# One change in four places of a fused attention block: sums moved between engines, sums left to DMA, transpositions moved later

## The chip, the cores and the metric

The kernel runs on one NeuronCore of a Trainium2 chip. The time is the device time of one execution in microseconds; lower is better. The core has five engines with instruction queues of their own, which run in order: TensorE (PE in the profile; its weight loads are PEld), VectorE (DVE), ScalarE (ACT), GpSimd (POOL) and SyncE (SP), which here only issues DMAs. GpSimd issues DMAs too. Both DMA queues share 16 DMA engines.

## The reference

For x of 2 batches x 1024 tokens x 1024 channels, all in float32:

```
xn  = layernorm(x)
qkv = clip(xn @ Wqkv.T, -8, 8);  q, k = layernorm(q)*w+b, layernorm(k)*w+b
att = softmax(q k' / sqrt(32) + slope_h * (kpos - qpos), causal) v     (32 heads of 32)
out = x + att @ Wout.T + xn @ (alpha * sign(Wffn)).T + bias
```

alpha is the mean of |Wffn| along a row.

## The kernel before

**Seven products.** Each 1024 x 1024 projection (k, q, v for each batch, and the output projection) is done for two token tiles of 128 at a time with seven products of blocks instead of eight. The weight matrix has blocks 11, 12, 21, 22 of 512 x 512, each held as 4 pieces (c = 0 to 3) of 128 x 512; from them come the sums t1 to t4 (`plan_difference`, L217 to L230). The token side has the quarters A11, A12 (first tile) and A21, A22 (second tile), and the sums S1 to S4 (`add_up`, L361 to L370: four operations of 128 x 512 on GpSimd). `seven` runs the blocks in the order 11, 21, t2, t3, t4, t1, 22: four accumulated matmuls each, with two records in the profile for one (L377). Blocks 11 and 21 need no sum of the second tile; t2 needs S2. `combine` adds the products up on VectorE (L396).

**Weights** go through a ring of 28 buffers of 128 x 512. A list `todo` holds loads, sums and stores in order; `load_weights(n)` gives it room for n more buffers, one after each matmul of the last pair of a projection. The first batch computes the sums (on GpSimd; t1 and t2 of the very first weights, k0, on VectorE) and stores them to DRAM right behind (`plan_store`, L236); the second batch loads them. The sums of Wout (o) are computed on GpSimd too, during the last tile of the binary layer.

**Pieces and sides.** `pieces()` yields the projections, the binary layer and the output projection in small pieces. Every second piece advances the generators in `sides`: normalizations (`layernorm`, `to_channels`, both with two empty yields between the last step of the normalization and the transposition on PE), the constants, and loads. `yield` thus fixes the distance in the queues, not in time.

**Attention** runs in 169 steps. A block is a batch, a half of the queries (qb = 0 or 1) and a group of four heads. For each block the first scores (L832) give the maximum of each query (VectorE, L849). `shifts` then has two halves: seven small GpSimd operations that make `shift_b` from the maxima (L865 to L871), and one step later four PE transpositions (`trs`, L876) and a ScalarE copy to `rows`. Nine steps behind, the second scores (L891, with `rows` added by L904) are masked on VectorE (L917), exponentiated on ScalarE (L926) and added up for the denominators on GpSimd (L942); the products with the values (L956) come one step later. A unit of second scores is one or two key tiles. A block of qb = 0 has 3 units and one of qb = 1 has 7; the first unit of a block has no sums on GpSimd, and the unit with two tiles (384 + 128 queries) has eight.

One step, as it stands in the program (L1039 to L1056): first scores; second half of `shifts` of the block that closed a step ago; first half of `shifts` of a block that closes now; division of a finished block (den, L975); pieces; products with the values; second scores; pieces. All engines run their queues in this order.

**The binary layer** (`binary_linear`) first takes |W| and sign(W) on ScalarE, two buffers ahead of the matmul that makes alpha (L601). Then for each of 16 token tiles: x and bias are added on GpSimd (L623), the product (L651) is scaled on VectorE to `fo` (L663), added to it on GpSimd in two halves (L664), and the row is stored to `out` (L666). The split of the tokens into two float32r parts needs two VectorE subtractions of SBUF operands for a tile (`hl`, L633). **The output projection** adds its rows to `out` with an adding DMA on GpSimd's queue (L725).

Of the kernel before, what the change touches and what calls it, by code (L numbers as in the profile page):

```python
# [25 lines left out]
def parallel_block_kernel(  # L26
# [36 lines left out]
    nc = tc.nc  # L63
# [134 lines left out]

    W = {}
# [17 lines left out]
    def plan_difference(what, to, a, b, c):  # L217


        def do():  # L220
            less = W[what, b, c]
            if to == "t3":
                w = W.pop((what, b, c))
            else:
                w = wpool.tile([P, HALF], FP, tag="w", name=f"w_{what}_{to}_{c}")
            eng = nc.vector if what == "k0" and to in ("t1", "t2") else nc.gpsimd
            eng.tensor_tensor(w, W[what, a, c], less, ALU.subtract)
            W[what, to, c] = w

# [11 lines left out]
    def plan_weights(what, src, e0, first, again):  # L241


        def part_of(block, c):
            r = ((int(block[0]) - 1) * NI + c) * P
            return src[r : r + P, e0 : e0 + D][:, half(int(block[1]) - 1)]

        if not first:
            for block in ORDER:
                for c in range(NI):  # L250
                    if block[0] == "t":
                        at = lambda name=f"{what[0]}{block}{c}": kept[name]
                    else:
                        at = part_of(block, c)
                    plan_load(what, block, c, at)
            return
        for block in ("11", "21"):
            for c in range(NI):
                plan_load(what, block, c, part_of(block, c))
        start = what == "k0"  # L260
        if start:
            for c in range(NI):
                for block in ("12", "22"):
                    plan_load(what, block, c, part_of(block, c))
        for c in range(NI + 2):
            if c < NI and not start:
                for block in ("12", "22"):
                    plan_load(what, block, c, part_of(block, c))
            if 0 < c <= NI:
                plan_difference(what, "t1", "12", "11", c - 1)  # L270
                plan_difference(what, "t2", "22", "t1", c - 1)
                plan_difference(what, "t3", "22", "12", c - 1)
            if again and c > 1:
                for to in ("t1", "t2", "t3"):
                    plan_store(what, to, c - 2)
        for c in range(NI + 1):
            if c < NI:
                plan_difference(what, "t4", "21", "t2", c)
            if again and c > 0:
                plan_store(what, "t4", c - 1)  # L280

    for b in range(B):
        for what, e0 in (("k", D), ("q", 0), ("v", 2 * D)):
            plan_weights(f"{what}{b}", wqkv_t, e0, b == 0, b == 0)
# [16 lines left out]
    plan_weights("o", wout_t, 0, True, False)  # L301
# [59 lines left out]
    def add_up(pr, eng, c0, c1):  # L361
# [5 lines left out]
        eng.tensor_tensor(at(S1), at(A21), at(A22), ALU.add)  # L367
        eng.tensor_tensor(at(S2), at(S1), at(A11), ALU.subtract)  # L368
        eng.tensor_tensor(at(S4), at(A12), at(S2), ALU.subtract)
# [21 lines left out]
    def combine(name, ra, rb, ready):  # L391

        h = {}

        def plus(dst, ps, other):
            nc.vector.tensor_tensor(dst, ps, other, ALU.add)  # L396

        def take(block, ps):
# [12 lines left out]
            elif block == "t1":  # L411
                plus(rb[:, half(1)], ps, h.pop("u3"))
                plus(h["u"], ps, h["u"])
# [53 lines left out]
    def turn_x(b, t):  # L467
# [13 lines left out]
        else:  # L481
            nc.gpsimd.dma_start(d[:, 0], pr[:, A21])
            add_up(pr, nc.gpsimd, 0, NI)
# [4 lines left out]
    def layernorm(b, t):  # L488
        yield from normalize_x(b, t)
        yield 0.0  # L490
        yield 0.0
# [9 lines left out]
    def to_channels(what, b, t, raw, par, at, d):  # L501
# [3 lines left out]
        yield 0.0  # L505
        yield 0.0
# [13 lines left out]
    def projected(what, b, ready):  # L520

        if what == "k":
            if b == 0:
# [5 lines left out]
                yield from normalize_x(b, 1)  # L529
            yield from turn_x(b, 0)  # L530
            if b == 0:
                load_weights(RING - 4 * NI)
        for p in range(NT // 2):
# [16 lines left out]
            yield from seven(pr, name, f"{what}{b}", not more, take, ORDER[:2])  # L550
            if what == "k":
                if p == 0:
                    yield from turn_x(b, 1)
                if more:
                    sides.append(layernorm(b, 2 * p + 3))
            assert ("x", b, p) in done
            yield from seven(pr, name, f"{what}{b}", not more, take, ORDER[2:])
# [8 lines left out]

    def values(b):
        def ready(t, rows):
# [9 lines left out]

    def binary_linear():
# [5 lines left out]
        ab = pair_tile("alpha_bias").rearrange("p k c q -> p (k c q)")  # L585
# [523 lines left out]
```

## Time and profile before

| | us |
|---|---|
| median of 3 runs | 1741.54 (1733.9 to 1747.48) |
| the profiled execution | 1737.78 |
| its span, first to last instruction | 1736.0 |
| PE busy | 1640.9 (95%) |
| GpSimd busy | 1052.9 (61%) |
| VectorE busy | 958.0 (55%) |
| ScalarE busy | 691.1 (40%) |
| DMA, mean over the span | 127 GB/s |
| mean granted clock of TensorE | 0.969 |

How the stages lie in the span: k, q and v of the first batch to about 365 us, without attention until 303; attention from there, with k, q and v of the second batch among it to 1005; magnitudes of the binary layer to 1050; its tiles to about 1365; the output projection to 1728. The profile gives for each engine its busy time, and for the idle time before an instruction what released it. Issuing a DMA is not counted as busy. A granted clock of 0.5 in a stretch means that PE ran at half speed for all of it. Records of PE are pipelined: a group of matmuls listed as 2.04 us x8 may hold overlapping ones.

### The profile page before, as it was taken

The page shows a single profiled execution, that of the slowest core. Times are in us where ns is not written, and L with a number is a line of the kernel's source. Part 1 is how long each engine was busy: PE and PEld are TensorE (multiplying, and loading weights), DVE is VectorE, ACT ScalarE, POOL GpSimd, SP SyncE. Part 2 cuts the span into 40 slices and gives each one's busy share as a digit, 9 for nine tenths or more (in the row PEclk, how much of TensorE's full clock was granted, in tenths as well). Part 3 has the DMA queues.
Part 4 walks back from the last instruction along what each step waited for, and adds up shares of the span by engine and source line. Part 5 has one row for each costly group of instructions (what it writes and reads, how often), then busy time and mean ns, then how long its engine had stood idle before and what let it go on. Part 6 is the DMA issues. An engine that isn't in the chain of part 4 may idle for free.

```text
span 1736.0 us, 25493 instructions
## 1 busy us (share of the span) xinstructions
PE 1640.9 (95%) x8480; PEld 691.5 (40%) x8480; DVE 958.0 (55%) x2782; ACT 691.1 (40%) x1425; POOL 1052.9 (61%) x1292
## 2 busy tenths in 40 slices
PE   3999999989999999999999998999989799999998
PEld 1444444433443333333333334545544333333343
DVE  4454352656666755666555556666776355555222
ACT  2442431125565445554433364444433243433420
POOL 7427043125654475557566667787887998777851
PEclk8999999999999999999999998899999899999999
DMA  7347475571325612336222434343332312331332
GB/s 285 146 160 270 134 245 183 188 268 66 141 74 178 222 59 76 104 104 224 61 80 98 152 134 151 111 134 121 133 106 86 103 28 77 97 74 20 87 59 48
DMA packets 108867, 220.83 MB, mean 127 GB/s; under 512 B 9856, under 2 KB 50304, under 8 KB 105664
## 3 DMA queue, kind: packets, MB, share of 16 engines
q1 hardware_dynamic: 87808, 139.24, 24.2%
q0 software_dynamic: 20928, 79.97, 14.2%
q8 instruction: 67, 1.10, 0.2%
q14 instruction: 64, 0.52, 0.1%
HBM read 139.74 MB, written 79.43 MB: 126 GB/s over the span
## 4 chain that ended last, share of the span: by engine, by line
PE 75%; DVE 8%; POOL 7%; issue 5%; ACT 3%; DMA 2%; SPq 0%; POOLq 0%; DVEq 0%; ACTq 0%
PE s L891 9%; PE s L832 9%; PE o L956 7%; PE mm_v_t L377 7%; PE mm_q_t L377 7%; PE mm_k_t L377 6%; PE mm_f L651 6%; PE mm_o_t L377 5%; PE mm_v L377 4%; PE mm_q L377 4%; PE mm_o L377 3%; POOL pT L942 2%; PE mm_k L377 2%; PE den L975 2%; PE s L904 2%
## 5 line engine op out<-in xcount | busy, mean ns | idle before, releaser
L942 POOL TENSOR_TENSOR pT<-pT,pT 128x512 f32<-128x512 f32 (+3 forms) x640 | 597.4, 958 | 171.0 <-ACT pT L926 160.3
L926 ACT ACTIVATE pT<-s,kpos 128x512 f32<-128x512 f32 (+3 forms) x768 | 379.6, 588 | 486.1 <-DVE s L917 287.1
L849 DVE CUSTOM_DVE_ANT_0 sumss<-s,rel 128x512 f32<-128x512 f32 (+3 forms) x512 | 302.3, 591 | 183.2 <-PE s L832 129.4
L832 PE MATMUL s<-kg,qg 32*128 32x512 f32 (+3 forms) x1536 | 206.4, 531 | 4.1 <-ACT pT L926 3.4
L891 PE MATMUL s<-qg,kg 32*128 32x512 f32 (+3 forms) x1536 | 196.5, 533 | 12.3 <-DVE mx L849 11.8
L917 DVE TENSOR_TENSOR s<-s,behind 128x128 f32<-128x128 f32 x512 | 123.8, 293 | 104.0 <-PE s L904 99.3
L956 PE MATMUL o<-pT,vg 128*32 128x512 f32 (+3 forms) x1536 | 159.9, 504 | 0.0
L651 PE MATMUL mm_f<-sg,hl 128*128 128x512 f32 x512 | 146.8, 426 | 2.8 <-ACT hl L630 2.4
L832 PEld LDWEIGHTS s<-kg,qg 32*128 32x128 f32 x1536 | 82.7, 186 | 129.9 <-issue 47.6
L891 PEld LDWEIGHTS s<-qg,kg 32*128 32x128 f32 x1536 | 76.0, 186 | 132.3 <-DVE mx L849 70.6
L377 PE MATMUL mm_k_t<-w_k_t,xT 128*128 128x512 f32 x224 | 110.1, 613 | 17.8 <-POOL xT L368 17.8
L989 POOL TENSOR_TENSOR o<-o,inv 128x512 f32<-128x512 f32 x31 | 39.4, 1272 | 139.9 <-ACT inv L984 139.8
L651 PEld LDWEIGHTS mm_f<-sg,hl 128*128 128x128 f32 x512 | 94.6, 197 | 63.2 <-issue 32.6
L377 PE MATMUL mm_q_t<-w_q_t,xp 128*128 128x512 f32 x224 | 107.6, 607 | 0.0
L377 PE MATMUL mm_v_t<-w_v_t,xp 128*128 128x512 f32 x224 | 106.1, 606 | 0.0
L377 PE MATMUL mm_k<-w_k,xT 128*128 128x512 f32 x192 | 99.3, 655 | 3.4 <-ACT xT L475 3.4
L849 DVE CUSTOM_DVE_ANT_0 umss<-s,rel,mx 128x512 f32<-128x512 f32 (+2 forms) x96 | 59.3, 617 | 63.1 <-PE s L832 52.6
L377 PE MATMUL mm_o_t<-w_o_t,ot 128*128 128x512 f32 x192 | 93.2, 610 | 0.0
L377 PE MATMUL mm_o<-w_o,ot 128*128 128x512 f32 x192 | 93.0, 612 | 0.0
L377 PE MATMUL mm_v<-w_v,xp 128*128 128x512 f32 x192 | 91.8, 611 | 0.0
L377 PE MATMUL mm_q<-w_q,xp 128*128 128x512 f32 x192 | 91.4, 604 | 0.0
L849 DVE CUSTOM_DVE_ANT_0 sumss<-s,rel,mx 128x512 f32<-128x512 f32 (+2 forms) x96 | 59.3, 617 | 48.2 <-PE s L832 37.7
(164 smaller groups left out, 1974.4 us busy)
## 6 DMA issues: line engine op xcount, KB each, us to landing
xp<-xd SPq DMA_DIRECT2D x16, 1792.0 KB, 7.6
kg<-kd SPq DMA_DIRECT2D x48, 256.0 KB, 4.8
vg<-vd SPq DMA_DIRECT2D x48, 256.0 KB, 5.1
xd<-xT POOLq DMA_DIRECT2D x8, 1280.0 KB, 4.9
x<-in_x_dram SPq DMA_DIRECT2D x16, 512.0 KB, 6.7
kd<-kT POOLq DMA_DIRECT2D x16, 512.0 KB, 4.1
qd<-qT POOLq DMA_DIRECT2D x16, 512.0 KB, 4.1
qg<-qd SPq DMA_DIRECT2D x32, 256.0 KB, 4.4
```

The lines of the kernel that those rows point to most:

```text
L377: nc.tensor.matmul(ps, pr[:, FACTOR[block], c, :], W[what, block, c], start=(c == 0), stop=(c == NI - 1),)
L651: nc.tensor.matmul(ps, hl[c // NI][:, m % 2, c % NI, :].bitcast(FR), sg[n, c], start=(m == 0), stop=(m == 2 * NC - 1),)
L832: nc.tensor.matmul(banks[j][:, c0 : c0 + n], q[r, tokens(i - qb * NQ)], k[r, :n], start=True, stop=True,)
L849: nc.vector.tensor_tensor_reduce(out=sums[:, :n], in0=banks[j][:, c0 : c0 + n], in1=rel[:, o0 : o0 + n], scale=1.0, scalar=LOWEST if k0 == ...
L891: nc.tensor.matmul(banks[j][:, c0:c1], k[r, tokens(kt % NQ)], q[r, q0:], start=(c0 == 0), stop=False,)
L904: nc.tensor.matmul(banks[j][:, c0:c1], ones_b[r, :], rows[r, q0:], start=False, stop=(c1 == HALF or (kt, q0) == unit[-1]),)
L917: nc.vector.tensor_tensor(at, at, behind, ALU.add)
L926: nc.scalar.activation(pT[:, c0:c1], banks[j][:, c0:c1], AF.Exp, bias=kpos[:, h, a : a + 1], scale=slopes[h],)
L942: nc.gpsimd.tensor_tensor(part_sum, part_sum, pT[:, c0:c1], ALU.add)
L956: nc.tensor.matmul(po[32 * j : 32 * j + 32, q0:], v[:, kt % NQ, 32 * j : 32 * j + 32], st["pT", name, j][:, c0:c1], start=opening, stop=la ...
L975: nc.tensor.matmul(ps[32 * j : 32 * j + 32, :], ones, st.pop(("sum", b, qb, g, j)), start=True, stop=True,)
L989: nc.gpsimd.tensor_tensor(ot, ot, inv, ALU.mult)
```

## The change

1. The sums change sign: weights are only added (t1 = 11 + 12, t2 = 22 + t1, t3 = 22 + 12, t4 = 21 + t2), and the token side and two of the combinations subtract instead. The number of operations stays.
2. The stores of k0's sums are put behind the first four loads of q0. Those of q0 and v0 stay.
3. The token sums of the very first pair go to VectorE. The second tile of a batch's first pair is transposed after block 11 instead of after 21, and the second tile's normalization comes after the first tile's transposition.
4. A third empty yield stands before the transpositions of normalized rows.
5. The sums of Wout are made in DRAM, by four copies and seven adding DMAs of 1 MB on GpSimd's queue, and all seven blocks are loaded.
6. x is copied to `out` by 16 DMAs on SP's queue, and bias is added by 16 adding DMAs on GpSimd's queue, both from the start of v0 on as a side; the binary layer's `fo` is added by 32 adding DMAs. x and bias are not loaded any more, and the additions L623 and L664 and the stores L666 go.
7. Magnitudes are taken three ahead, into larger buffers.
8. In the last block, the sums of key tiles 5 to 7 go to VectorE.
9. In each step both halves of `shifts` come after the second scores.

```diff
@@ plan_difference, now plan_sum
-            eng.tensor_tensor(w, W[what, a, c], less, ALU.subtract)
+            eng.tensor_tensor(w, W[what, a, c], more, ALU.add)
@@ plan_weights, now plan_first (batch 0) and plan_again (batch 1 and o)
+        start = what == "k0"
         for block in ("11", "21"):
             for c in range(NI):
-                plan_load(what, block, c, part_of(block, c))
+                put(block, c)
+            while later:
+                plan_store(*later.pop(0))
...
-            if again and c > 1:
+            if c > 1:
                 for to in ("t1", "t2", "t3"):
-                    plan_store(what, to, c - 2)
+                    later.append((what, to, c - 2))
+            while later and not start:
+                plan_store(*later.pop(0))
...
-    plan_weights("o", wout_t, 0, True, False)
+    plan_again("o", wout_t, 0)
@@ add_up
-        eng.tensor_tensor(at(S1), at(A21), at(A22), ALU.add)
+        eng.tensor_tensor(at(S1), at(A21), at(A22), ALU.subtract)
         eng.tensor_tensor(at(S2), at(S1), at(A11), ALU.subtract)
-        eng.tensor_tensor(at(S4), at(A12), at(S2), ALU.subtract)
+        eng.tensor_tensor(at(S4), at(A12), at(S2), ALU.add)
@@ turn_x
-            add_up(pr, nc.gpsimd, 0, NI)
+            add_up(pr, nc.vector if (b, p) == (0, 0) else nc.gpsimd, 0, NI)
@@ layernorm and to_channels
-        yield 0.0
-        yield 0.0
+        for _ in range(3):
+            yield 0.0
@@ projected
                 yield from normalize_x(b, 0)
-                yield from normalize_x(b, 1)
             yield from turn_x(b, 0)
             if b == 0:
+                yield from normalize_x(b, 1)
                 load_weights(RING - 4 * NI)
...
-            yield from seven(pr, name, f"{what}{b}", not more, take, ORDER[:2])
-            if what == "k":
-                if p == 0:
-                    yield from turn_x(b, 1)
-                if more:
-                    sides.append(layernorm(b, 2 * p + 3))
+            args = pr, name, f"{what}{b}", not more, take
+            yield from seven(*args, ORDER[:1])
+            if what == "k" and p == 0:
+                yield from turn_x(b, 1)
+            yield from seven(*args, ORDER[1:2])
+            if what == "k" and more:
+                sides.append(layernorm(b, 2 * p + 3))
@@ new: a side, appended at the start of values(0)
+    def beside():
+        yield from residual()
+        yield from output_weights()
+    def residual():
+        for b, t in every_tile:
+            nc.sync.dma_start(out[b, tokens(t), :], x[b, tokens(t), :])
+            yield 0.0
+        for _ in range(12):
+            yield 0.0
+        for b, t in every_tile:
+            nc.gpsimd.dma_start(
+                out[b, tokens(t), :], bias.partition_broadcast(P), accum_op=ALU.add
+            )
+            yield 0.0
+            yield 0.0
+    def output_weights():
+        parts = {
+            "t1": ("11", "12"),
+            "t2": ("22", "11", "12"),
+            "t3": ("12", "22"),
+            "t4": ("21", "22", "11", "12"),
+        }
+        full = {}
+        for n in range(4):
+            for to, of in parts.items():
+                if n >= len(of):
+                    continue
+                src = block_of(wout_t, 0, of[n])
+                if n == 0:
+                    full[to] = dram.tile([HALF, HALF], FP, tag=f"wo{to}", name=f"wd_o{to}", bufs=1)
+                    nc.gpsimd.dma_start(full[to], src)
+                else:
+                    nc.gpsimd.dma_start(full[to], src, accum_op=ALU.add)
+                yield 0.0
+            for _ in range(8):
+                yield 0.0
...
@@ binary_linear
-        magnitude(0)
-        magnitude(1)
+        for a in range(3):
+            magnitude(a)
...
-            xr = io_tile(f"xr_{b}_{t}")
-            nc.sync.dma_start(xr, x[b, tokens(t), :])
             yield 0.0
-            nc.gpsimd.tensor_tensor(xr, xr, bias_bc, ALU.add)
...
                 nc.vector.tensor_tensor(fo, ps, alpha[:, half(n)], ALU.mult)
-                nc.gpsimd.tensor_tensor(xr[:, half(n)], xr[:, half(n)], fo, ALU.add)
+                nc.gpsimd.dma_start(out[b, tokens(t), half(n)], fo, accum_op=ALU.add)
                 yield SHORT
-            nc.gpsimd.dma_start(out[b, tokens(t), :], xr)
@@ second_scores
-                nc.gpsimd.tensor_tensor(part_sum, part_sum, pT[:, c0:c1], ALU.add)
+                late = (b, qb, g) == blocks[-1] and kt > NT // 2
+                eng = nc.vector if late else nc.gpsimd
+                eng.tensor_tensor(part_sum, part_sum, pT[:, c0:c1], ALU.add)
@@ the main loop
-        for c in chains:
-            next(c, None)
-        chains = []
-        if n in closes:
-            chains.append(shifts(*closes[n]))
-            next(chains[-1])
         m = n - LAG
...
             second_scores(*second[m])
+        for c in chains:
+            next(c, None)
+        chains = []
+        if n in closes:
+            chains.append(shifts(*closes[n]))
+            next(chains[-1])
         fill(free * (1.0 - BEFORE))
```

## The prediction

> **What bounds the kernel now.** I read the page first: TensorE (PE) is busy for 95% of the span, the next engine, GpSimd (POOL), for 61%. So the change can win only what PE loses: its stops, and half clock after them. The chain of waits, for PE alone, gives the stops:
>
> ```profile
> PE mm_k_t L377 <- POOL xT L368: 17.8, 2, 14.8
> PE tr_x L448 <- ACT x L443: 13.9, 5, 8.3
> PE s L891 <- DVE mx L849: 11.8, 8, 3.9
> PE den L975 <- POOL pT L942: 11.3, 1, 11.3
> PE trs L876 <- POOL shift_b L869: 10.6, 5, 5.7
> PE ps_a L601 <- ACT absw L592: 5.7, 3, 2.6
> ```
>
> Columns: total us, times, longest. One stop of 14.8 us is the token sums of the first pair; 11.3 us is a denominator waiting for a GpSimd queue that had fallen behind. The table of stretches of 50 us then says where GpSimd is the limit (columns: length, busy PE, PEld, DVE, ACT, POOL, clock, DMA share, GB/s):
>
> ```profile
> 1250.00:1300.00 50.00, 44.33 (x290) 22.22 (x291) 36.95 (x90) 22.14 (x42) 44.35 (x43) 0.97 0.36 127
> 1300.00:1350.00 50.00, 46.10 (x268) 22.35 (x268) 30.56 (x68) 17.56 (x32) 40.82 (x38) 0.89 0.24 80
> 1350.00:1400.00 50.00, 38.66 (x228) 15.05 (x226) 19.41 (x56) 14.72 (x29) 48.02 (x52) 0.86 0.31 101
> ```
>
> GpSimd works 41 to 48 us of each 50, and PE has its worst stretches there, at a lowered clock. Last the timeline, around one closing block of the first batch:
>
> ```profile
> 871.85 0.40 PE L904 MATMUL s<-rows,ones_b 3*128 3x384 bf16 x8
> 874.92 6.02 POOL L942 TENSOR_TENSOR pT<-pT,pT 128x384 f32<-128x384 f32 x8
> 876.92 0.40 PE L876 MATMUL trs<-ident_b,shift_b 128*128 128x128 bf16 x4
> 880.56 0.29 PE L904 MATMUL s<-rows,ones_b 3*128 3x256 bf16 x4
> ```
>
> A step's second scores end at 872.25, its eight sums on GpSimd at 880.94, the next step's second scores at 880.85. Remember these three times.
>
> **First pair's sums: -12.5 us.** PE stands from 26.66 to 41.44, because GpSimd does the 16 weight stores, the k0 sums and constants first, and S1 and S2 (1.27 us each) only from 38.78. Now VectorE does them. What is late next: the copies of the second tile's transposition on ScalarE, which queue behind the third tile's Ln at 23.48 (0.29), its Exp (0.20) and one PSUM copy (0.58), so they end at about 25.8. The four t4 sums on GpSimd, no longer parted by stores, fill about 22.3 to 27.4, and a VectorE sum of two SBUF operands can wait such a run out (shown below at line 633), so S2 ends near 28.8 (0.69 each). 41.4 - 28.9 = 12.5; bounds -16 (no waiting) and -9 (another GpSimd run).
> The 16 stores move to the first loads of q0 (120 to 140 us), where DMA is already busy for its whole time (share 0.99 and 1.04 in two stretches of 10 us). 4 MB more at 360 to 390 GB/s are 11 us; q0's t2 sums end 4 us before PE wants them, the t4 sums are just in time: **+3** (0 to +7).
>
> **Transpositions a yield later: -5 us.** The stops at 70, 72, 100, 101, 155, 255 and 260 us, together 5.5 us, wait for a normalized row (bounds 0 and -5.5). Behind them only the sums for the next pair come later, with 9 us to spare.
>
> **Residual and bias in DRAM: +4 us.** 16 copies on SP's queue fit in the empty DMA slices at 290 to 300 and 320 to 330. The 16 bias adds on GpSimd's queue fall at about 316 to 370. An adding DMA of 512 KB lands in 5.2 us against 3.2 for a plain one (rows out_dram from or and from xr), and its 4096-byte packets take 397 ns in the mean in the last 60 us, plain ones 160: 128 x 0.397/16 = 3.2 us of all engines each. k1's 7 MB of weights and its x tiles load at 340 to 370, at a DMA share of 0.86 to 1.0; PE already stops 5.0 us there. Moving the second tile's transposition one block forward helps by up to 5; late loads cost up to 15. I take +4, by the row of the full DMA. The eleven 1 MB DMAs for Wout come at about 370 to 560 (share 0.36 over the first batch), needed after 1005: nothing; if GpSimd had to wait for one, up to 3 us each inside the same bound.
>
> **Magnitudes three ahead: -4 us** of the 5.7 us of ps_a and the 10.2 us at half clock from 1044.7 (5.1 lost; bounds 0 and -8).
>
> **GpSimd relieved, 1050 to 1400 us: -33 us.** Out go the bias sum (16 x 2.49 = 39.8 us), the residual sum (32 x 1.33 = 42.5), 16 stores (9.2) and 16 Wout sums (16 x 1.27 = 20.3); in come 32 adding DMAs at the 0.86 us of line 725 (27.5): 84 us less. What PE loses there:
>
> ```profile
> 1333.01 8.44 DVE L633 TENSOR_TENSOR hl<-xt,hl 128x512 fp32r<-128x512 f32 x2
> 1333.03 2.37 POOL L623 TENSOR_TENSOR xr<-xr,alpha_bias 128x1024 f32<-128x1024 f32 x1
> 1335.37 4.93 POOL L942 TENSOR_TENSOR pT<-pT,pT 128x512 f32<-128x512 f32 x4
> 1341.91 1.85 PE L891 MATMUL s<-qg,kg 32*128 32x512 f32 x2 [3.90 <-DVE mx L849]
> ```
>
> Two subtractions that take 0.68 each alone stand 8.4 us while GpSimd runs, then PE waits 3.9. Stops of this kind: 3.42, 0.90, 1.53, 3.90 and the denominator's 11.34, 21.1 together; half clock follows them for 10.2, 6.8, 3.4, 6.8 and 13.7 us, a loss of half, 20.5. Of 41.6 I take 80%, since runs of four or eight sums (5 to 6 us) stay (bounds -41 and -17). A half-tile fo is now free only when its DMA has landed: 0.86 + 5.2 us, under the 19 us until its buffer returns.
>
> **The main loop's chain: +51 us.** Both halves of `shifts` move behind `second_scores`. So the seven small GpSimd operations (2.1 us from 865's start to the last 869's end) stand behind that step's sums, and PE's transposition behind the next step's second scores. In the block shown: sums end 880.94, shift_b 883.0, PE is there at 880.5: it stands 2.5 us. It is in order; behind it wait the next fills and scores, and ScalarE's copy of rows. I worked this for all 32 blocks, with the step's own sums: blocks of the first half of the queries follow an opening unit without sums and have 5 to 14 us to spare. The first batch's eight late blocks stand 1.8, 0.1, 1.9, 2.9, 0, 2.5, 1.8, 2.4; the two after them 0.5, 0.8; the second batch's, with GpSimd's backlog taken out up to 1365 us, 1.6, 2.0, 2.8, 2.6, 3.2, 3.0, 4.9, 7.0 (the last two behind four sums of `add_up`). 42 in all, for today's 10.6: +31.
> Then the clock. Stops of 2.4 us and more here are followed by half clock six times in seven, shorter ones from 1 us four times in ten, mostly for 6.8 us. Nine long and five short ones of the eighteen: 9 x 0.85 x 3.4 + 5 x 0.4 x 3 = 32, less today's 5, and rounded down since three of the twelve slow stretches last only 3.4 us: **+20**. Bounds of the whole: 0 (shift_b in time, by the rows of the early blocks) and +74 (42 - 10.6 + 14 x 3.4 - 5).
>
> ```profile
> 408.38 1.53 PE L891 MATMUL s<-qg,kg 32*128 32x512 f32 x3 [1.06 <-DVE mx L849]
> ```
>
> ```profile
> 410.00:417.00 7.00, 7.00 (x14) 2.18 (x15) 4.11 (x15) 3.55 (x5) 2.27 (x8) 0.53 0.45 188
> ```
>
> After a stop of 1.06 us (timeline) the granted clock is 0.53 of full speed for 7 us (table of stretches). The Trainium skill ("TensorE: Matmul & The Clock Gate", "HAM oscillation — how this bites in real kernels") gives as its rule that gaps longer than about 3.4 us are to be avoided. By that rule only two stops of the chain would slow the clock, its term would be about +2 instead of +20, and the sum 18 us lower; the row speaks against it.
>
> **Last sums on VectorE: 0.** The last denominators at 1675.47 follow a matmul without a stop, and GpSimd's sums end at 1671.36. 12 sums by 0.69 fit; behind GpSimd runs they could cost 3.
>
> **Sum.** -12.5 + 3 - 5 + 4 - 4 - 33 + 51 = +3.5 on the profiled execution's 1737.8 (span 1736.0), so 1741.3. The median of the runs, 1741.5, lies 3.8 above that execution: **1745 us** as such a median.
>
> **Rivals.**
> A, slower: the stop at shift_b with its clock. Place: PE's transposition in the 18 blocks with sums ahead. Price: all fourteen stops over 1 us pay 3.4 us of clock, 48 instead of 25, so +23: 1768 (own range 1759 to 1795, as the stops themselves may be a third longer). From a chain cost of 65 us on it decides for slower by over 1%. For it: six of seven long stops did pay. Against: nine of the eighteen are under 2.4 us.
> B, faster: GpSimd, relieved, and VectorE, quicker at the masks that the exponentials wait for, bring shift_b in time; the chain costs nothing: 1694. For it: two of the first eight late blocks hardly stop as it is. Against: 6.0 of the 8.7 us from scores to sums are GpSimd's own time.
> C, the change does not do what it says: adding DMAs starve k1's loads (+15 in place of +4) and the late release of fo keeps VectorE waiting (a third of the 33 lost): 1767.
>
> **Chances.** Forecast 0.40 (its own range 1727 to 1763), A 0.28, B 0.24, C 0.08. Within 1% (1724 to 1759), about what a measurement of this kernel can tell from no change, lie most of the forecast, 0.26, and 0.07 of the others. Faster by over 1%: B's 0.22 and 0.07 of the forecast. Slower: A's 0.26, C's 0.05 and 0.07. The range must reach into A and B: 1694 to 1785 leaves half of B and a quarter of A out.
>
> **What would show it.** Right: PE's stop at mm_k_t near 12 us shorter; no POOL line 623 or 664; denominators without a long stop at 1350 to 1400; waits "trs from shift_b" of 30 to 45 us in some 16 places, with a clock under 1.0 in the stretches from 600 to 1000, where it is 1.00 now. Wrong: trs waits as small as today's (B), or a DMA wait at 365 to 390 (C).

## The result, and the profile after

The changed kernel takes 1793.9 us (median of four runs, 1788.2 to 1798.3), the kernel before in the same comparison 1739.1 us (1733.9 to 1747.5): a ratio of 1.031 [1.025, 1.037]. It is 55 us slower, where 1745 was forecast with a range of 1694 to 1785. The profiled execution has a span of 1796.5 us with a mean granted clock of 0.954; before it was 1736.0 us and 0.969. The difference of the two spans, 60.5 us, is what has to be explained.

The waits of TensorE come first, as before (total us, times, longest):

```profile
PE trs L939 <- POOL shift_b L932: 43.2, 16, 7.3
PE s L895 <- ACT rows L941: 30.6, 1, 30.6
PE mm_k_t L390 <- DVE xT L381: 10.6, 1, 10.6
PE mm_q_t L390 <- POOL w_q_t L228: 8.5, 4, 4.3
PE tr_x L467 <- ACT x L462: 8.4, 1, 8.4
PE mm_v_t L390 <- POOL w_v_t L228: 5.7, 3, 3.4
```

The first line is the chain's stop, forecast as 42 us in 16 places. The second is new and is one single stop; the prediction had named a DMA wait at about that place, but only as the sign of its rival C. The third is the first pair's stop. It was to become some 12 us shorter and became 4.2 us shorter, but it ends 11.1 us earlier (at 30.3 us in place of 41.4), since the matmuls ahead of it end earlier too. The waits for w_q_t and w_v_t stand at the beginning of q0 and of v0 and are new. The wait of tr_x is the one at the very start, which stood before as well (8.3 us); the seven short stops before transpositions that were forecast to go, 5.5 us together, are gone. So is the wait for a denominator (11.3 us before).

Where GpSimd was the limit, it now has room. These are the stretches of 1250 to 1400 us of the changed kernel (length, busy PE, PEld, DVE, ACT, POOL, clock, DMA share, GB/s), beside which POOL stood at 44, 41 and 48 before:

```profile
1250.00:1300.00 50.00, 48.05 (x353) 25.97 (x352) 34.48 (x106) 22.50 (x49) 31.22 (x46) 1.00 0.42 113
1300.00:1350.00 50.00, 47.94 (x287) 22.46 (x289) 33.65 (x82) 19.39 (x36) 31.14 (x29) 0.93 0.34 73
1350.00:1400.00 50.00, 45.95 (x306) 23.41 (x299) 28.63 (x80) 18.13 (x32) 34.72 (x40) 0.93 0.40 91
```

The timeline at one closing block of the first batch shows the chain's new place:

```profile
807.71 5.38 POOL L1007 TENSOR_TENSOR pT<-pT,pT 128x128 f32<-128x128 f32 x7
813.04 0.23 POOL L928 TENSOR_TENSOR sh<-mx,pos 128x16 f32<-128x16 f32 x1
814.95 0.25 POOL L932 CAST shift_b<-sh 128x16 bf16<-128x16 f32 x1
815.26 0.41 PE L939 MATMUL trs<-ident_b,shift_b 128*128 128x128 bf16 x4 [2.72 <-POOL shift_b L932]
815.90 0.60 ACT L941 COPY rows<-trs 128x512 bf16<-128x512 bf16 x1
```

The sums end (the stretch opens behind the first of the eight), then come the seven small operations, 2.2 us long, of which the first and the last are shown, and TensorE, which had finished its second scores at 812.5, waits 2.7 us for the last of them.

The long stop is read in the stretches from 250 to 400 us, where v0 ends and k1 begins. First the kernel before, then the changed one:

```profile
250.00:300.00 50.00, 48.34 (x125) 21.91 (x124) 18.09 (x31) 10.15 (x24) 22.89 (x27) 1.00 0.63 216
300.00:350.00 50.00, 50.00 (x173) 21.14 (x172) 32.51 (x103) 4.91 (x9) 5.59 (x18) 1.00 0.54 187
350.00:400.00 50.00, 44.70 (x234) 20.47 (x233) 26.97 (x93) 14.41 (x29) 15.73 (x25) 1.00 0.60 218
```

```profile
250.00:300.00 50.00, 44.20 (x110) 19.51 (x109) 13.86 (x23) 9.61 (x22) 20.77 (x26) 0.93 0.95 362
300.00:350.00 50.00, 47.81 (x163) 20.13 (x162) 30.03 (x94) 4.91 (x9) 14.51 (x25) 1.00 0.90 231
350.00:400.00 50.00, 23.27 (x92) 10.79 (x90) 11.43 (x32) 1.07 (x2) 6.67 (x13) 0.79 1.01 262
```

The DMA share (the column before the last) goes from between 0.54 and 0.63 to between 0.90 and 1.01, which is all engines busy nearly all the time, while the engines' busy time falls by half and more in the last stretch. The chain of work that ended last says, in order of time, who waits for whom there:

```profile
356.19 25.48 DMA w_k_t<-wd_kt
381.73 13.00 DMA w_k_t<-wd_kt
...
395.62 5.85 DMA x<-in_x_dram
...
403.06 0.30 ACT rstd_x L451
...
403.49 0.58 ACT rows L941
404.11 1.22 PE s L895 x2
```

The chain runs through k1's weight loads for 38 us. SP issues the tile x only behind them, at 395.6 us; VectorE's statistics of that tile had waited for it for 30.4 us; ScalarE has the Ln of that tile ahead of its copy of `rows`, and TensorE's next scores need `rows`. Each of these queues runs in order here, so one late load stands in front of everything. For 30.7 us from 378.6 us on the granted clock is half, but all but the last 5 us of that lie within the stop (373.5 to 404.1 us) and cost little beyond it. The DMA issues of 310 to 410 us give the transfers (KB each, median us from issue to landing):

```profile
out_dram<-in_bias_dram POOLq DMA_DIRECT2D x16, 512.0 KB, 18.5
w_k_t<-wd_kt SPq DMA_DIRECT2D x16, 256.0 KB, 18.6
```

The bias add was priced at 5.2 us; the weight load took 4.0 us before, between 300 and 410 us.

### The profile page after: what moved, and what is told of

Read it like the earlier page. It is cut to its first block, busy times and chain, and to the rows that moved or that the text cites. A ratio compares the mean times of both kernels' runs of the same rounds, so it can differ in the third digit from the quotient of the medians.

```text
span 1796.5 us, 25513 instructions
## 1 busy us (share of the span) xinstructions
PE 1655.4 (92%) x8480; PEld 699.3 (39%) x8480; DVE 951.2 (53%) x2798; ACT 693.5 (39%) x1425; POOL 984.4 (55%) x1254
## 4 chain that ended last, share of the span: by engine, by line
PE 68%; POOL 9%; DMA 8%; DVE 7%; issue 5%; ACT 2%; SPq 0%; POOLq 0%; DVEq 0%; ACTq 0%
PE s L954 8%; PE s L895 8%; PE mm_f L715 7%; PE o L1021 6%; PE mm_q_t L390 6%; PE mm_k_t L390 5%; POOL pT L1007 5%; PE mm_v_t L390 5%; PE mm_o_t L390 4%; PE mm_q L390 4%; PE mm_o L390 3%; PE mm_k L390 3%; PE mm_v L390 3%; DMA w_k_t<-wd_kt 2%; DMA x<-in_x_dram 2%
## 5 line engine op out<-in xcount | busy, mean ns | idle before, releaser
L1007 POOL TENSOR_TENSOR pT<-pT,pT 128x512 f32<-128x512 f32 (+2 forms) x628 | 593.0, 976 | 192.2 <-ACT pT L989 182.2
L895 PE MATMUL s<-kg,qg 32*128 32x512 f32 (+3 forms) x1536 | 210.4, 528 | 36.5 <-ACT rows L941 30.6
L954 PE MATMUL s<-qg,kg 32*128 32x512 f32 (+3 forms) x1536 | 189.4, 527 | 5.7 <-DVE mx L912 5.1
L390 PE MATMUL mm_o_t<-w_o_t,ot 128*128 128x512 f32 x256 | 128.5, 635 | 0.0
L390 PE MATMUL mm_k_t<-w_k_t,xT 128*128 128x512 f32 x224 | 110.1, 613 | 10.6 <-DVE xT L381 10.6
L390 PE MATMUL mm_v_t<-w_v_t,xp 128*128 128x512 f32 x224 | 112.3, 634 | 6.1 <-POOL w_v_t L228 5.7
L390 PE MATMUL mm_q<-w_q,xp 128*128 128x512 f32 x192 | 96.6, 639 | 0.3 <-DVE mx L912 0.3
```

What stands on the lines that cost most here:

```text
L390: nc.tensor.matmul(ps, pr[:, FACTOR[block], c, :], W[what, block, c], start=(c == 0), stop=(c == NI - 1),)
L895: nc.tensor.matmul(banks[j][:, c0 : c0 + n], q[r, tokens(i - qb * NQ)], k[r, :n], start=True, stop=True,)
L954: nc.tensor.matmul(banks[j][:, c0:c1], k[r, tokens(kt % NQ)], q[r, q0:], start=(c0 == 0), stop=False,)
L1007: eng.tensor_tensor(part_sum, part_sum, pT[:, c0:c1], ALU.add)
```

## The experiments

Three theories stood at the start: the chain's place and the adding DMAs at the handover from v0 to k1 share the loss (theory 1), the handover and the start carry nearly all of it (theory 2), or the chain alone does (theory 3). In what follows a time is a median, and a ratio is to the kernel before, measured on the same chip. The runs were made on three chips, on which the kernel before took 1741.0, 1740.3 and 1741.3 us.

**undo_chain: the change without its chain.**

```diff
 # ahead of the weighing of values and the second scores, as before
+        for c in chains:
+            next(c, None)
+        chains = []
+        if n in closes:
+            chains.append(shifts(*closes[n]))
+            next(chains[-1])
...
             second_scores(*second[m])
-        for c in chains:
-            next(c, None)
...
```

> The changed kernel with one part undone: the chain of the shifts (both halves) stands again ahead of the weighing of values and the second scores, all else as changed. Theory 1 (two costs, the chain's place and the adding DMAs at the handover from v0 to k1, share the loss): the trs waits fall from 43 us in 16 places to under 11 us, the half clock behind them goes, and the time falls by 40 to 60 us against the changed kernel's 1794, to 1734-1754, about the kernel before; the stop of 30 us at 374 to 404 us stays. Theory 2 (the handover and the start cost nearly all of it, the chain's stops only move waits): the time falls by under 20 us, 1775 or more. Theory 3 (the chain alone is the loss): 1700 or less, since first pair and GpSimd's relief gain some 45 us.

Measured: 1728.3 us, 0.993 [0.991, 0.994]. The chain's place costs 66 us here, somewhat more than theory 1 gave it (40 to 60) and less than theory 3 (94 or more); without it the change is a small gain. The two longest waits of this kernel, and what is left of the chain's:

```profile
PE mm_k L390 <- ACT u_k L420: 29.2, 1, 29.2
PE mm_k_t L390 <- DVE xT L381: 9.5, 1, 9.5
...
PE trs L939 <- POOL shift_b L932: 4.0, 3, 2.7
```

The stop at 371 to 400 us is still there in full (now at another instruction behind the same Ln on ScalarE): it has nothing to do with the chain. So both causes exist.

**chain_alone: the kernel before with the chain moved, and nothing else.**

```diff
-        for c in chains:          # ahead of the second scores
...
             second_scores(*second[m])
+        for c in chains:
+            next(c, None)
+        chains = []
+        if n in closes:
+            chains.append(shifts(*closes[n]))
+            next(chains[-1])
```

> The kernel before with the chain of the shifts alone moved behind the second scores. Theory 1: GpSimd is still loaded with the bias and residual sums there, so the trs waits are at least those of the changed kernel (43 us and more, in about 18 places) and the time rises by 45 to 75 us over 1739, to 1784-1814. Theory 2: it rises by less than 20 us.

Measured: 1788.2 us, 1.027 [1.025, 1.029]: 47 us more than the kernel before. The trs waits are 47.8 us in 16 places, 37 more than before. Other stops shrink by it: the denominator's goes from 11.3 to 2.3 us. My reading, which no run tests, is that a TensorE that waits for GpSimd at the transposition finds it less behind later, so that the chain alone costs less than its 66 us in the changed kernel, which has no such backlog.

**no_bias and bias_last: the bias adds left out, and put behind the Wout DMAs.**

```diff
 # no_bias: residual() ends with the 16 copies of x
-        for b, t in every_tile:
-            nc.gpsimd.dma_start(
-                out[b, tokens(t), :], bias.partition_broadcast(P), accum_op=ALU.add
-            )
...
 # bias_last: the adds, as a function of their own, come last
         yield from output_weights()
+        yield from bias_adds()
```

> The changed kernel without the 16 adding DMAs of the bias (the bias is left out of the output; the 16 copies of x to the output and the eleven Wout DMAs stay). Theory 1: the stop of 30.6 us at the first scores behind ACT's rows (374 to 404 us) and the half clock for the 30.7 us after it are the adds' doing, so both go: 35 to 50 us less than the changed kernel's 1794, 1744-1759. Rival (the copies and the DRAM-to-DRAM traffic of Wout starve the loads as well): the stop shrinks but 10 us or more of it stay, 1765-1780. Rival (the stop comes from the order on SP's queue and ScalarE's, not from the adds): the stop stays at 25 us or more.

> The changed kernel with nothing left out: the 16 adding DMAs of the bias start behind the eleven Wout DMAs, two steps apart as before, so at some 500 to 600 us, in the first batch's attention, in place of 310 to 370 us. Theory 1: at 373 us there is no stop over 10 us, and the later adds meet a DMA share of 0.3 to 0.5 and so cost under 8 us: 1745-1765. Rival (such an add costs wherever it stands, its 512 KB needing 18 us of landing): a new stop at the adds' new place, over 10 us in all, and 1770 or more.

Measured: no_bias 1781.6 us, 1.023 [1.021, 1.025]; bias_last 1782.5 us, 1.024 [1.022, 1.027]. Both are only 11 to 12 us less than the changed kernel, and both expectations of theory 1 missed. The stop shrinks to 17.4 and 19.1 us. The reason is in the DMA issues of no_bias from 310 to 405 us:

```profile
wd_ot<-in_wout_t_dram POOLq DMA_DIRECT2D x7, 1024.0 KB, 22.4
w_k_t<-wd_kt SPq DMA_DIRECT2D x16, 256.0 KB, 13.9
```

With the bias adds gone from their place, the 1 MB DMAs for Wout move up into it: the generator yields them next. They are issued from 285 to 367 us here and from 284 to 366 us in bias_last, in place of 412 to 555. This is what the first rival of no_bias said, that the traffic for Wout starves the loads as well. So these two runs exchange one set of adding DMAs for another. They don't clear the handover, and say only that it is not the bias adds as such.

**side_late: nothing but the copies in the handover** (on top of undo_chain).

```diff
         yield from residual()            # the 16 copies only
+        while ("k", 1) not in done:
+            yield 0.0
         yield from output_weights()
+        yield from bias_adds()
```

> The changed kernel with the chain put back (the kernel of the run undo_chain, 1728.3 us), and with the eleven Wout DMAs and then the 16 bias adds begun only when the keys of the second batch are done (past 500 us); the 16 copies of x stay in v0. Theory 1 (all the adding DMAs between 310 and 410 us, bias and Wout together, hold up k1's weights and x tiles): the stop of 29 us at 371 to 400 us goes but for 5 us, and with the half clock behind it 30 to 45 us are gained: 1683-1698. Rival (the copies, which take the idle DMA slices at 256 to 300 us and push vd's stores and k1's loads back, are the cause): a stop of 10 us or more stays there, 1705-1720. Rival (the adds cost the same at any place): 1720-1730.

Measured: 1703.2 us, 0.979 [0.977, 0.981], 25 us less than undo_chain. This is 5 us above the interval that theory 1 gave, and below the rivals' ones. The stretches of side_late, to be held against the two sets above:

```profile
300.00:350.00 50.00, 49.68 (x174) 20.86 (x173) 30.09 (x95) 4.90 (x9) 5.60 (x18) 1.00 0.56 191
350.00:400.00 50.00, 45.54 (x210) 21.25 (x209) 29.93 (x101) 13.74 (x28) 14.53 (x24) 0.97 0.63 224
```

DMA share, TensorE and clock are nearly back at the kernel before; the stop is 4.2 us in place of 29.2, and these 25 us are as much as the whole gain. The adds that were moved to 800 to 950 us cost nothing that shows there (TensorE is busy for 149.7 us of the 150, before for 149.4), and land sooner, at a DMA share of 0.69:

```profile
out_dram<-in_bias_dram POOLq DMA_DIRECT2D x16, 512.0 KB, 7.3
```

**no_residual: side_late without the copies and the bias adds.**

```diff
-        for b, t in every_tile:
-            nc.sync.dma_start(out[b, tokens(t), :], x[b, tokens(t), :])
-            yield 0.0
...
-        yield from bias_adds()
```

> The kernel of side_late without the copies of x and without the bias adds (x and the bias are left out of the output); the Wout DMAs stay late. Theory 1: the same handover as in side_late, so within 8 us of it. Rival (copies): 10 to 25 us faster than side_late, with no stop over 5 us between 300 and 410 us.

Measured: 1694.8 us, 0.975 [0.973, 0.976], 8.4 us less than side_late, just outside what theory 1 allowed (8) and below what the rival asked for (10). 6.4 us of that are gained before the first transposition of a block (335.0 us in side_late, 328.6 us here). In undo_chain, with the copies, the stores of v0's weight sums landed in 13.2 us (240 to 300 us); here they land in 2.8 us, and the stops at mm_v_t (5.4 us in side_late) go. The bias adds, which this run leaves out as well, have no part in that: in side_late they begin at 803 us. So the copies that were to fit into idle slices cost some 6 us too.

**stores_behind: k0's 16 stores right behind their sums** (on top of undo_chain).

```diff
-            while later and not start:
+            while later:
                 plan_store(*later.pop(0))
```

> The kernel of undo_chain with k0's 16 weight stores right behind their sums again, ahead of the first pair's work on GpSimd's queue, in place of between q0's first loads. Theory 1: the waits of mm_q_t for w_q_t (9.0 us in 5 places) fall to under 2 us, and what follows them; the start stop at mm_k_t, whose sums are on VectorE now, grows by under 3 us (the four t4 sums of GpSimd come later by the stores' 9 us, so VectorE's sums are less disturbed, but PE's first t4 blocks may wait): 3 to 12 us faster than undo_chain, 1716-1725. Rival (the stores ahead hold up the t4 weights that PE needs next): slower than undo_chain, 1730-1740.

Measured: 1729.0 us, 0.994 [0.992, 0.996], the same as undo_chain; both expectations missed. The waits for w_q_t shrink from 9.0 to 2.8 us, and as much comes back at the start, where there are two stops now:

```profile
PE mm_k_t L390 <- DVE xT L381: 7.3, 1, 7.3
PE mm_k_t L390 <- DVE xT L383: 6.5, 1, 6.5
```

q0's first matmul is at 138.3 us in place of 130.9, v0's at 245.8 in place of 247.4. The move of the stores is neutral: 7 us won at the start, 9 lost in q0.

**first_on_gpsimd: the first pair's sums back on GpSimd** (on top of undo_chain).

```diff
-            add_up(pr, nc.vector if (b, p) == (0, 0) else nc.gpsimd, 0, NI)
+            add_up(pr, nc.gpsimd, 0, NI)
```

> The kernel of undo_chain with the first pair's four sums on GpSimd as in the kernel before; the stores stay moved to q0's loads. Theory 1 (both the stores' move and VectorE's speed shorten the start): GpSimd is free of the stores, so S1 and S2 (1.27 us each) begin at about 27 us and end near 31: 2 to 4 us slower than undo_chain, 1730-1733. Rival (GpSimd's t4 sums and constants still stand ahead): the stop goes back to 13 us or more, 1733-1738.

Measured: 1733.9 us (1728.1 to 1740.2), 0.997 [0.995, 0.998]: about 6 us more than undo_chain, on medians of runs that overlap. The stop is 12.6 us in place of 9.5. Of the 15.1 us by which q0 begins earlier in undo_chain than before (130.9 us, 146.0), VectorE's part is 4.4 (135.3 here), and 7.4 came from the stores' move (138.3 in stores_behind). The other 3 were not tried by themselves; the first matmul of k0 stands 3.2 us earlier in all these kernels, without the 3.1 us wait for its tokens (`mm_k` from ACT xT) that it had before.

**late_chain and second_half_late: which half of the chain costs** (both on top of side_late).

```diff
 # second_half_late
+        fresh = []
+        if n in closes:
+            fresh.append(shifts(*closes[n]))
+            next(fresh[-1])               # GpSimd's half, ahead of the sums
...
             second_scores(*second[m])
+        for c in chains:                  # TensorE's half, behind the scores
+            next(c, None)
+        chains = fresh
```

> The kernel of side_late (1703.2 us) with the chain behind the second scores again, as in the change. Undoing the chain gained 66 us in the changed kernel, putting it alone into the kernel before cost 47. Theory 1a (the 66 is the chain's own price where GpSimd and DMA are as in the change, 43 us of trs waits and their half clock): 1760-1775. Theory 1b (some 20 us of the 66 came from the chain and the busy DMA queues of 310 to 560 us together): 1745-1757, with trs waits of 40 us or more all the same.

> The kernel of side_late with only the second half of the chain (TensorE's four transpositions and ScalarE's copy of rows) behind the second scores of the next step; the first half, GpSimd's seven small operations, stays ahead of that step's sums. Theory 1 (the price comes from GpSimd's half, which stands behind eight sums in its queue; TensorE's half only moves the point at which it is needed): trs waits fall from 4.0 us to under 2 us, and the time is that of side_late within 6 us, 1697-1707. Rival (the transposition behind the second scores delays rows, and with them the next block's scores, whatever GpSimd does): 15 us or more slower, with waits for rows in place of shift_b.

Measured: late_chain, with both halves behind the second scores as in the change, 1763.0 us, 1.013 [1.010, 1.016], 60 us above side_late. Theory 1a holds: the price is the chain's own, and needs no busy DMA queues.

```profile
PE trs L943 <- POOL shift_b L936: 45.9, 17, 7.3
```

second_half_late: 1703.9 us, 0.979 [0.976, 0.981], the time of side_late, without a trs wait in the list. So TensorE's half costs nothing behind the scores. All of the price comes from GpSimd's seven small operations standing behind that step's sums, as the prediction's times said (sums end at 880.94, shift_b at 883.0, TensorE is there at 880.5).

**gpsimd_load: GpSimd's old work put back as sums that nobody reads** (on top of side_late).

```diff
+            nc.gpsimd.tensor_tensor(spare, spare, other, ALU.add)
...
+                nc.gpsimd.tensor_tensor(spare[:, half(n)], spare[:, half(n)], fo, ALU.add)
                 nc.gpsimd.dma_start(out[b, tokens(t), half(n)], fo, accum_op=ALU.add)
```

> The kernel of side_late with GpSimd's old work of the output tiles put back as sums whose result nobody reads: for each tile one 128x1024 sum in place of the bias sum and two 128x512 sums behind fo in place of the residual's; the output is unchanged. Theory (GpSimd's relief was worth what it was priced at, 33 us between 1050 and 1400 us): 25 to 42 us slower than side_late, 1728-1745, all of it between the first output tile and the end of the last. Rival (the gain from 1050 to 1400 us came from the magnitudes or from ScalarE and DMA): under 12 us slower.

Measured: 1735.0 us, 0.996 [0.995, 0.998], 32 us above side_late. The relief was priced at 33. The time from the first matmul of the output tiles (mm_f) to the first of the output projection grows from 290.6 to 323.9 us, so the loss lies where it was forecast. Two stretches show it at work, with POOL at 45 to 46 us of 50 again and a TensorE that stops in the second:

```profile
1250.00:1300.00 50.00, 50.00 (x337) 25.30 (x335) 35.10 (x97) 23.80 (x47) 45.20 (x42) 1.00 0.36 84
1300.00:1350.00 50.00, 39.33 (x257) 19.16 (x251) 35.74 (x64) 17.10 (x32) 45.80 (x47) 0.92 0.32 69
```

**all_late: the copies moved too** (on top of side_late).

```diff
-        yield from residual()
-        while ("k", 1) not in done:
+        while ("x", 1, 1) not in done:
             yield 0.0
+        yield from residual()             # copies two steps apart
         yield from output_weights()
         yield from bias_adds()
```

> The kernel of side_late with the 16 copies of x moved as well: copies, Wout DMAs and bias adds all begin when the second pair of the second batch is turned (past 420 us), the copies two steps apart. Theory 1: the copies' 6 us at 250 to 330 us (vd's and the weights' stores landing in 13 us in place of 3) go, and the DMAs meet idle slices: 1694-1700. Rival (the copies, issued on SP's queue among the loads of keys and values, hold those up): 1705 or more.

Measured: 1693.8 us, 0.973 [0.970, 0.975]: 47 us faster than the kernel before and 100 us faster than the changed kernel, with nothing left out. Its stretches, and behind them the last one in the kernel before:

```profile
250.00:300.00 50.00, 49.54 (x134) 22.30 (x132) 17.31 (x28) 9.61 (x22) 20.78 (x27) 1.00 0.59 204
300.00:350.00 50.00, 49.68 (x174) 21.03 (x167) 30.83 (x100) 4.90 (x9) 5.07 (x17) 1.00 0.63 214
350.00:400.00 50.00, 45.36 (x238) 20.82 (x236) 27.82 (x97) 15.87 (x33) 17.74 (x28) 0.93 0.57 204
...
600.00:800.00 200.00, 197.29 (x1091) 73.83 (x1084) 120.14 (x357) 99.49 (x206) 134.08 (x148) 1.00 0.67 165
```

```profile
600.00:800.00 200.00, 197.29 (x1086) 74.35 (x1086) 119.31 (x352) 102.36 (x213) 116.22 (x130) 1.00 0.32 106
```

The same DMAs are now issued from 398 to 840 us (copies to 537, Wout from 545 to 683, bias from 709), where the DMA share rises (0.67 in place of 0.32 at 600 to 800 us) and TensorE is as busy as in the kernel before (197.3 us of 200 in both).

## Why the prediction was wrong

It forecast no change that a measurement can tell, and the kernel became 3% slower. Its steps, one by one, with measured places taken from the traces (mostly the first matmul of a stage) or from two medians:

| step of the prediction | priced | measured | from |
|---|---|---|---|
| first pair's sums; transpositions later | -17.5 | -14.1 | q0 begins at 131.9 us, before 146.0 |
| k0's stores in q0 | +3 | +11.6 | q0 to v0: 116.4 us, before 104.8 |
| residual, bias and Wout in DRAM | +4 | +34.5 | undo_chain less all_late, 1728.3 - 1693.8 |
| magnitudes three ahead | -4 | +1.3 | first ps_a to first mm_f: 35.7 us, before 34.4 |
| GpSimd relieved | -33 | -38.8 | first mm_f to the end of the last mm_o, all_late 639.4, before 678.2 |
| main loop's chain | +51 | +65.7 | changed kernel less undo_chain, 1793.9 - 1728.3 |

The measured column adds up to +60, and the spans differ by 60.5; that the two agree so well is partly luck, as medians and single traces are mixed in it, and as the piece behind the last matmul, 2.1 us longer in the changed kernel, is left out.

**The step that failed** is "Residual and bias in DRAM: +4 us", with its words "late loads cost up to 15. I take +4" and, for Wout, "nothing". The mechanism was seen: it is rival C, and the prediction named a DMA wait at 365 to 390 us as its sign. Its price, +4, was about a ninth of the 34.5 us that it came to, and even rival C's +15 was less than half. Moving these DMAs shows where the 34.5 us come from; why the price was so low is an argument from the traces. Two things were left out of the sum, and both could have been read in the profile of before.

First, demand. The prediction had worked out 3.2 us of all 16 DMA engines for each bias add, so 51 us for the sixteen. The DMA share at 300 to 400 us was 0.54 and 0.60, so 57 us of those 100 were taken. 57 + 51 is more than 100: the loads had to be late. It compared the add's own landing time (5.2 us) and the full share (0.86 to 1.0 at 340 to 370 us) one after the other and didn't add them up. With the adds the shares became 0.90 and 1.01.

Second, order. A late load was priced as a delay of itself, "up to 15". But the loads stand in SP's queue ahead of the x tile, that tile's Ln stands in ScalarE's queue ahead of `rows`, and VectorE's statistics of the same tile stand ahead of its maxima. One late tile kept VectorE, ScalarE and TensorE standing for 30 us and more (30.4, 34.6 and 30.6). This order is read from the chain of waits; no run changed it by itself. Moving the adds gave 25 us (undo_chain to side_late), moving the copies the other 9 (side_late to all_late).

The Trainium skill ("DMA: Bandwidth & Descriptors", "Queues, rings and completion order") states that a DMA engine with work in several queues takes turns among them, one packet at a time. The rows of 300 to 410 us, packets, MB and share of 16 engines, do not speak against it. First the kernel before, then the changed one:

```profile
q1 hardware_dynamic: 7776, 15.21, 40.6%
q0 software_dynamic: 1456, 6.03, 13.8%
```

```profile
q0 software_dynamic: 3392, 12.32, 53.2%
q1 hardware_dynamic: 7248, 14.95, 40.2%
```

SP's queue (q1) got the same time on the engines as before, and its packets took hardly longer (0.402 x 16 x 110 / 7248 = 0.10 us, before 0.09). So the loads were late by waiting, not by moving more slowly. GpSimd's queue (q0) took nearly four times its former share, at 0.532 x 16 x 110 / 3392 = 0.28 us a packet. If a turn is one packet of these rows, which no run shows, the loads get the smaller part of the time for as long as both queues have work. No run here tells such turns from plain want of time.

**k0's stores** were mis-sized: +3 became +11.6, though the move won 7 us at the start that the prediction had booked under the first pair. By stores_behind the two cancel: 9.0 of the 11.6 us go when the stores move back. The bound was +7; the 11 us of extra transfer, which the prediction had worked out for a stretch of full DMA, would have been nearer.

**The chain** was right in mechanism, place and size of its stops: 42 us forecast in about 16 places, 43.2 in 16 measured. The second batch's eight late blocks were forecast at 1.6, 2.0, 2.8, 2.6, 3.2, 3.0, 4.9 and 7.0 us and stood 1.6, 4.1, 2.5, 1.7, 3.3, 3.1, 5.8 and 7.3. What was off is the base. 10.6 us of stops were taken off as today's, of which 6.6 go with GpSimd's relief anyway (undo_chain has 4.0 left); with these moved, the terms read -40 and +58 against -39 and +66 (+60 in late_chain).

On the clock: from side_late to late_chain the stops grow by 42 us and the mean granted clock of the profiled executions falls from 0.973 to 0.965. By span times the missing share, 1708.5 x 0.027 = 46 and 1762.8 x 0.035 = 62, that is 16 us lost. Between undo_chain (1726.1 us, 0.969) and the changed kernel (1796.5 us, 0.954) it is 29 us. Single executions differ by as much: that of side_late is its slowest, and its four lose between 36 and 46 us. Medians over the four executions of each kernel give 24 us in both comparisons (37 to 62, and 54 to 79). This counts half clock during stops as lost, so it is a bound from above. The prediction's +20 was about right; the longer stops (42 and 39 us more) and this clock account for about the 60 and 66.

The Trainium skill's rule on gaps over about 3.4 us ("TensorE: Matmul & The Clock Gate", "HAM oscillation — how this bites in real kernels") made the term about +2: three of the trs stops of late_chain are longer than that, and three of the changed kernel's. But in the changed kernel half clock of 3.4 us or more begins also at seven of its thirteen shorter trs stops, those of 1.62, 2.21, 2.46, 2.54, 2.72, 2.75 and 3.32 us, and the loss is some 24 us. The measurement decides against using the rule as a threshold.

**The rest.** GpSimd's relief was right in place and size, and gpsimd_load shows its cause (32 us). In its working the size is in part luck: half clock that lies within a stop was counted besides the stop, most of all at the denominator, whose 13.7 us of half clock begin 9.5 us before its stop ends, so that the 41.6 us were some 5 too many. The first pair's stop moved as forecast: the t2 block begins at 30.3 us in place of 41.4. The magnitudes gained nothing: the wait for them shrank from 5.7 to 4.7 us, but the stop for the first hl behind them grew from 2.4 to 4.3. The last sums on VectorE were not tried by themselves. Of the rivals, A (the chain costs more) and C happened together: with +34.5 in place of +4 the forecast would have been 1775, and with the chain's +66 in place of +51 as well it would have been 1790. Either alone would have left the time within the stated range.

## What to carry to other kernels

Before a transfer is put into a stretch, add its time on all DMA engines to the share that is already taken there. If the sum is over the stretch's length, expect the loads of that stretch to be late, as here, and price not the transfer but everything that stands in order behind the latest load. A side task with no due date belongs where the DMA share is low, not where the program happens to reach it; the same DMAs cost 34 us more at one place than at another, where the copies and the bias adds cost nothing that shows (all_late takes no longer than no_residual, which has neither).

When work is moved past another step, ask for each engine's half separately what it now queues behind: TensorE's half of this chain could move for nothing, GpSimd's could not.

## What the runs showed of the hardware that was not expected

An adding DMA's landing time depends on its surroundings more than on itself: the same 512 KB bias add landed in 18.5 us at a DMA share of 0.90 to 1.01 and in 7.3 us at a share of 0.69; plain 256 KB weight loads beside it went from 4.0 to 18.6 us.

Half clock does not need a long stop: in the changed kernel it begins at seven of thirteen stops for shift_b that are shorter than 3.4 us, the shortest of them 1.62 us, and in the kernel before it followed one of 1.06 us.

Delays on GpSimd partly hide one another. The moved chain cost 47 us in the kernel that had GpSimd's backlog and 60 to 66 us where the backlog was gone, and in the former the wait for a denominator fell from 11.3 to 2.3 us. That the chain's stops let GpSimd catch up is argued from these numbers, not shown.
